# Four graph layers in one kernel: the softmax denominators of layer 0 carried by transfers instead of a matmul, and another order of the opening

## The chip, the cores and the metric

The kernel runs on one core of a Trainium2 chip. A core has TensorE (PE: matmuls, with PEld for its weight loads), VectorE (DVE), ScalarE (ACT), GpSimd (POOL) and SyncE (SP), each with its own instruction stream, executed in order, and 16 DMA engines that all queues share. The streams meet only through semaphores. The metric is device time in microseconds (us) for one execution. Lower is better.

## The reference

`x` is 4096 x 256, `adj` is a 4096 x 4096 weighted adjacency matrix, in which most entries are zero. Four layers follow one another, each with a residual and a layer norm:

```python
x = _layernorm(x + attention(x, adj))      # layer 0: 4 heads of 64, below
x = _layernorm(x + gat(x, adj))            # layer 1: masked softmax over neighbours
x = _layernorm(x + gcn(x, adj))            # layer 2: normalized adj @ x @ W.T + b
x = _layernorm(x + relu(gcn3(x, adj)))     # layer 3
# layer 0, per head:
scores = q @ k.T * HD ** -0.5 + graph_bias * adj
scores = where(adj == 0, -1e9, scores)
attn   = exp(scores - max) / sum(exp(scores - max))
out    = attn @ v            # heads side by side, then @ Wout + bout
```

The change concerns layer 0 alone. All data are float32, except a bfloat16 copy of the adjacency that layer 0 writes for layer 1.

## The kernel before, in words

Layer 0 treats the queries in 32 blocks of 128 rows (class `Rows`) and each block in two units, one per pair of heads (class `Pair`). A unit takes 4 steps of 1024 keys each, so there are 64 units and 256 steps. The function `step(t)` writes out by hand what each engine does in step t; inside `manual_schedule` the order of the program is the order on each engine. A software pipeline lays the stages of a unit over several steps. In step t:

- `score` (L366, PE): the scores of the current unit into two PSUM tiles `sc`; DVE adds the bias and takes the row maximum (`z`, L375).
- `expo` (L391, ACT): exponentials of the unit four steps back, with the row sums collected in `ls`.
- `turn` (L405, PE; copied out by ACT, L413): the exponentials are transposed by TensorE, five steps back.
- `attend` (L423, PE): values times transposed exponentials, six steps back, into the PSUM tile `po`: 64 channels of head 0 on partitions 0 to 63, of head 1 on 64 to 127, queries along the free axis.
- `make_bias` and `make_edges`: for the next block of queries, DVE turns a tile of the adjacency (`raw`, loaded by SP in four transfers, L256) in 32 x 32 blocks (L272) and makes the bias from it (L277, L278); ACT makes the bfloat16 copy (L289) and POOL sends it to DRAM (`edge`, L295). There are two `raw` buffers.

With `ka` for the step of the unit that attends (0 to 3), a unit ends like this. The sums lie one per partition (a query is a partition in `ls`), but `po` has the queries along the free axis, so the reciprocals must be turned and repeated over 64 partitions. In step ka = 2 `sums` reduces `ls`, takes the reciprocals and spreads them over 64 columns each (`lb`, L437, DVE). In step ka = 3, after `attend`, `norm` multiplies `lb` by the identity on TensorE (L441) into a PSUM tile `pb`, which DVE copies to `rb` (L449). At the start of the next step (ka = 0 of the next unit) `scale` multiplies `po` by `rb` into `oT` (L452). For every second unit, step ka = 1 runs `finish`: output projection (L335), residual and layer norm statistics on DVE (L345, L113, L114). `begin` makes the queries of the next block (L313, PE; L321, DVE; L329, POOL) in step ka = 0 of every second unit. `po`, `pb`, the pq of `begin` and the pp of `finish` all live in two PSUM tiles, tags `po0` and `po1`.

The opening comes before step 0 and overlaps steps 0 to 3. The eight blocks of 512 rows of x are projected to keys and values by `project`: keys (L210, PE, evicted by ACT, L217), then values (L226, PE, evicted by DVE, L233). The bias of block 0 is made from four `raw` tiles. Both must have been done for the first scores. The program calls `begin` first, then interleaves the whole bias of block 0 with `project(0)` and `project(1)`, and projects two blocks at the start of each of the steps 1 to 3, ahead of the scores.

Of the kernel before, what the change touches and what calls it, by code (L numbers as in the profile page):

```python
# [16 lines left out]
P = 128  # L17
# [27 lines left out]
def tile_gnn(  # L45
# [59 lines left out]
    sc = [ps_q.tile([P, TS], F32, name=f"sc{j}") for j in range(2)]  # L105

    edge = dram.tile([N, N], BF16, name="edge")
    off_diag = const.tile([P, P], F32, name="off_diag")
    nc.vector.tensor_scalar(off_diag, ident, -1.0, 1.0, ALU.mult, ALU.add)

# [58 lines left out]
    with ExitStack() as l0:  # L169
# [31 lines left out]
            )  # L201
            x_in[mb] = xt

        def project(mb):

            xt = x_in.pop(mb)
            for pr in range(2):
                pk = ps_o.tile([P, 512], F32, tag=f"po{pr}", name="pk")
                for cc in range(2):
                    nc.tensor.matmul(  # L210
                        pk,
                        wkv_sb[:, cc, pr * P : (pr + 1) * P],
                        xt[:, cc, :],
                        start=(cc == 0),
                        stop=(cc == 1),
                    )
                nc.scalar.activation(  # L217
                    kT[:, pr, mb * 512 : (mb + 1) * 512],
                    pk,
                    AF.Identity,  # L220
                    bias=bqk_sb[:, 2 + pr : 3 + pr],
                )
            pv = ps_t.tile([P, 4, D], F32, tag="tr", name="pv")
            for s in range(4):
                for cc in range(2):
                    nc.tensor.matmul(  # L226
                        pv[:, s, :],
                        xt[:, cc, s * P : (s + 1) * P],
                        wkv_sb[:, cc, D : 2 * D],
                        start=(cc == 0),  # L230
                        stop=(cc == 1),
                    )
            nc.vector.tensor_tensor(  # L233
                v_sb[:, mb * 4 : (mb + 1) * 4, :],
                pv,
                bv_b.unsqueeze(1).to_broadcast([P, 4, D]),
                ALU.add,
            )
            if mb + 4 < N // 512:
                load_x(mb + 4)  # L240

        class Rows:

# [64 lines left out]
            def begin(self, tag):  # L308
                self.qT = wk2.tile([P, 2, P], F32, tag="qT", name="qT")
                pq = ps_o.tile([P, 512], F32, tag=tag, name="pq")  # L310
                for pr in range(2):
                    for cc in range(2):
                        nc.tensor.matmul(  # L313
                            pq[:, pr * P : (pr + 1) * P],
                            wq_sb[:, cc, pr * P : (pr + 1) * P],
                            self.xq[:, cc, :],
                            start=(cc == 0),
                            stop=(cc == 1),
                        )
                for pr in range(2):  # L320
                    nc.vector.tensor_scalar(  # L321
                        self.qT[:, pr, :],
                        pq[:, pr * P : (pr + 1) * P],
                        bqk_sb[:, pr : pr + 1],
                        HD ** -0.5,
                        ALU.add,
                        ALU.mult,
                    )
                nc.gpsimd.tensor_tensor(self.xr, self.xr, bout_b, ALU.add)  # L329
                self.oT = wk2.tile([P, 2, P], F32, tag="oT", name="oT")  # L330

            def finish(self, tag):
                pp = ps_o.tile([P, 512], F32, tag=tag, name="pp")
# [16 lines left out]
        class Pair:  # L350
# [79 lines left out]

            def sums(self):

                l2 = wk2.tile([P, 2], F32, tag="l2", name="l2")
                nc.vector.tensor_reduce(l2, self.ls, AX.X, ALU.add)
                nc.vector.reciprocal(l2, l2)
                self.lb = wk2.tile([P, 2, HD], F32, tag="lb", name="lb")
                nc.vector.tensor_copy(self.lb, l2.unsqueeze(2).to_broadcast([P, 2, HD]))  # L437

            def norm(self, tag):
                pb = ps_o.tile([P, 512], F32, tag=tag, name="pb")  # L440
                nc.tensor.matmul(  # L441
                    pb[:, 0:P],
                    self.lb.rearrange("p j d -> p (j d)"),
                    ident,
                    start=True,
                    stop=True,
                )
                self.rb = wk2.tile([P, P], F32, tag="rb", name="rb")
                nc.vector.tensor_copy(self.rb, pb[:, 0:P])  # L449

            def scale(self):
                nc.vector.tensor_tensor(  # L452
                    self.rows.oT[:, self.pr, :], self.po[:, 0:P], self.rb, ALU.mult
                )
# [7 lines left out]
        def step(t):  # L462
# [10 lines left out]
            grow = live and ib + 1 < NCH  # L473
            if grow and pr == 0 and k == NS - 1:
                rows[ib + 1].fetch()
            if ua > 0 and ka == 0:
                pairs[ua - 1].scale()
            if t > 0:
                for mb in range(2 * t, min(2 * t + 2, N // 512)):
                    project(mb)  # L480
            if live:
                if k == 0:
                    pairs[unit] = Pair(rows[ib], pr)
                pairs[unit].score(k)
            if expos:
                pairs[ue].expo(ke, 0)
            if turns:
# [3 lines left out]
            if attends:  # L491
                pairs[ua].attend(ka, tag_a)
                if ka == NS - 2:
                    pairs[ua].sums()
                if ka == NS - 1:
                    pairs[ua].norm(tag_o)
            if ua > 0 and ka == 1:
                if ua % 2 == 0:
                    pairs[ua - 1].rows.finish(tag_o)
                del pairs[ua - 1]  # L500
            if grow:
                if pr == 1 and k == NS - 2:
                    rows[ib + 1].begin(tag_o if attends else "po1")
                kb, half = divmod(pr * NS + k, 2)
                if edges:
                    edges.pop().make_edges()
                edges.append(rows[ib + 1])
                rows[ib + 1].make_bias(kb, half)
                if half == 0 and kb + 1 < NS:
                    rows[ib + 1].load(kb + 1)  # L510
                elif half == 0 and ib + 2 < NCH:
                    rows[ib + 2].load(0)
# [1 line left out]
                edges.pop().make_edges()  # L514
            if turns:
                pairs[ut].turn(kt, 1, by_dve=not live)
            for f, *args in tail.get(t, ()):
                f(*args)

# [97 lines left out]
        def first_es():  # L617
# [30 lines left out]
                (first_es,),  # L648
            ],
        }  # L650
        with tc.manual_schedule():
            load_x(0)
            nc.sync.dma_start(wkv_sb, wqkv[:, D:].rearrange("(c p) e -> p c e", p=P))
            rows[0].load(0)
            load_x(1)
            rows[0].load(1)
            rows[0].fetch()
            load_x(2)
            load_x(3)
            nc.scalar.dma_start(wout_sb, wout.rearrange("(c p) e -> p c e", p=P))  # L660
            nc.scalar.dma_start(bout_b, bout.partition_broadcast(P))
            rows[0].begin("po1")
            for k in range(NS):
                for half in range(2):
                    rows[0].make_bias(k, half)
                    rows[0].make_edges()
                if k < 2:
                    project(k)
                if k + 2 < NS:
                    rows[0].load(k + 2)  # L670
                elif k + 2 == NS:
                    rows[1].load(0)
            for t in range(n_steps + LA + 2):
                step(t)

# [444 lines left out]
```

## Time and profile before

| | |
|---|---|
| median of 3 runs | 2788.17 us (2787.74 to 2789.93) |
| the profiled execution, its own time | 2790.52 us |
| its span, first to last instruction | 2788.7 us |
| PE busy | 2720.9 us, 98% |
| DVE busy | 2225.5 us, 80% |
| ACT busy | 1655.4 us, 59% |
| POOL busy | 234.3 us, 8% |
| layer 0, roughly | 0 to 1436 us |

The page gives busy time by engine, the span in slices, the chain of work that ended last, and the costliest groups of instructions with what ended the idle time ahead of them. A timeline lists instructions with start and duration; a row of several instructions is merged. The end of a matmul is modelled, so where TensorE does one thing after another, the time from one start to the next is the safer measure.

### The profile page before, as it was taken

What the parts mean: (1) busy time and instruction counts of PE and PEld (TensorE: products, weight loads), DVE (VectorE), ACT (ScalarE), POOL (GpSimd) and SP (SyncE); (2) the same over time, 40 slices, a digit from 0 to 9 for tenths busy, and PEclk for the clock granted to TensorE, in tenths of its full rate; (3) what the DMA queues carried; (4) which work ended last, traced back from release to release, by engine and by line L of the source; (5) the groups of instructions that cost most, each with busy time, mean ns of one, the idle gap of its engine ahead of it and who ended that gap; (6) DMA issues with size and microseconds to landing.
All of it is one profiled execution on the core that took longest, in us unless ns stands there. A gap on an engine that the chain in (4) does not pass through costs nothing.

```text
span 2788.7 us, 57962 instructions
## 1 busy us (share of the span) xinstructions
PE 2720.9 (98%) x23568; PEld 1862.4 (67%) x23568; DVE 2225.5 (80%) x4059; ACT 1655.4 (59%) x2675; POOL 234.3 (8%) x404
## 2 busy tenths in 40 slices
PE   6999999999999999999997999999999999999997
PEld 4677777777777777777786888886444444444443
DVE  4799999999988999999858888885866577676565
ACT  2699999999999999999857777772100001000000
POOL 1111111111111111111100000000200000000000
PEclk9999999999999999999999999999999999999998
DMA  6344444444444444444362222212555555555552
GB/s 156 63 83 86 93 87 85 89 90 83 87 92 83 88 89 84 90 87 87 95 202 70 77 77 76 76 43 90 176 158 170 162 159 157 164 168 175 181 169 73
DMA packets 671291, 308.01 MB, mean 110 GB/s; under 512 B 547376, under 2 KB 577456, under 8 KB 671024
## 3 DMA queue, kind: packets, MB, share of 16 engines
q1 hardware_dynamic: 655776, 265.10, 38.7%
q0 software_dynamic: 13440, 37.77, 3.5%
q8 instruction: 184, 3.01, 0.5%
q10 hardware_dynamic: 1808, 1.44, 0.2%
q14 instruction: 83, 0.68, 0.1%
HBM read 258.21 MB, written 46.01 MB: 109 GB/s over the span
## 4 chain that ended last, share of the span: by engine, by line
PE 93%; issue 3%; DVE 1%; DMA 1%; ACT 1%; SPq 0%; POOL 0%; DVEq 0%; POOLq 0%; ACTq 0%
PE m L948 27%; PE po L423 17%; PE po L770 16%; PE sc L366 16%; PE ptr L405 10%; PE py L982 2%; PE pq L313 1%; PE pp L335 1%; PE pb L441 1%; PE pk L210 1%; PE pv L226 1%; DMA mk<-edge 1%; SPq L256 0%; DMA x<-xs 0%; DVE z L375 0%
## 5 line engine op out<-in xcount | busy, mean ns | idle before, releaser
L375 DVE CUSTOM_DVE_ANT_0 z<-sc,bias 128x1024 f32<-128x1024 f32 x512 | 605.9, 1221 | 40.5 <-PE sc L366 39.0
L391 ACT ACTIVATE z<-z,nm 128x1024 f32<-128x1024 f32 x512 | 590.2, 1153 | 6.7 <-DVE nm L387 6.7
L413 ACT COPY pt<-ptr 128x1024 f32<-128x1024 f32 x507 | 511.4, 1009 | 99.3 <-PE ptr L405 89.9
L366 PE MATMUL sc<-store,qT 64*128 64x512 f32 x2048 | 506.7, 608 | 1.6 <-DVE mx L375 1.5
L423 PE MATMUL po<-pt,xc 128*64 128x128 f32 x8192 | 504.2, 276 | 0.0
L770 PE MATMUL po<-store,pt 128*128 128x257 f32 x2048 | 447.2, 380 | 12.6 <-issue 12.6
L423 PEld LDWEIGHTS po<-pt,xc 128*64 128x64 f32 x8192 | 442.3, 137 | 17.6 <-DVE pt L411 0.2
L405 PEld LDWEIGHTS ptr<-ident,z 64*128 64x128 f32 x8192 | 322.3, 138 | 177.8 <-issue 78.4
L770 PEld LDWEIGHTS po<-store,pt 128*128 128x128 f32 x2048 | 388.6, 190 | 70.9 <-issue 12.7
L948 PE MATMUL m<-asum,ysum 128*128 128x512 f32 x768 | 356.6, 594 | 6.3 <-issue 6.3
L405 PE MATMUL ptr<-ident,z 64*128 64x64 f32 x8192 | 356.3, 225 | 5.8 <-ACT pt L413 4.4
L366 PEld LDWEIGHTS sc<-store,qT 64*128 64x128 f32 x2048 | 192.9, 189 | 119.4 <-issue 109.2
L948 PEld LDWEIGHTS m<-asum,ysum 128*128 128x128 f32 x768 | 146.0, 190 | 177.9 <-issue 160.9
L948 PE MATMUL m<-asum,store 128*128 128x512 f32 x512 | 263.2, 596 | 0.0
L948 PE MATMUL m<-a,ysum 128*128 128x512 f32 x512 | 245.9, 594 | 0.0
L295 POOL DMA_DIRECT2D edge<-mk x256 | 145.4, 568 | 1004.5 <-ACT mk L289 981.1
L954 ACT COPY e<-m 128x512 f32<-128x512 f32 x32 | 18.5, 586 | 351.6 <-PE m L948 351.6
L917 DVE TENSOR_TENSOR asum<-a 128x512 f32<-128x512 f32 x128 | 88.1, 688 | 163.9 <-PE m L948 163.9
L724 ACT ACTIVATE z<-z,es_q 128x1024 f32<-128x1024 f32 x128 | 146.5, 1145 | 120.5 <-DVE mx L711 111.9
L278 DVE SCALAR_TENSOR_TENSOR bias<-rt,gb,u 128x512 f32<-128x512 f32 x256 | 194.2, 759 | 9.1
L760 DVE STREAM_TRANSPOSE pt<-z 128x1024 f32<-128x1024 f32 x128 | 158.1, 1237 | 41.7 <-PE po L770 41.7
L948 PEld LDWEIGHTS m<-asum,store 128*128 128x128 f32 x512 | 97.8, 191 | 123.3 <-issue 121.4
(123 smaller groups left out, 2561.5 us busy)
## 6 DMA issues: line engine op xcount, KB each, us to landing
a<-in_adjT SPq DMA_DIRECT2D x256, 512.0 KB, 5.1
raw<-in_adjT SPq DMA_DIRECT2D x512, 128.0 KB, 4.0
edge<-mk POOLq DMA_DIRECT2D x256, 128.0 KB, 2.5
mk<-edge SPq DMA_DIRECT2D x256, 128.0 KB, 2.9
xt<-in_xT SPq DMA_DIRECT2D x8, 512.0 KB, 5.4
xq<-in_xT SPq DMA_DIRECT2D x32, 128.0 KB, 3.9
xr<-in_x SPq DMA_DIRECT2D x32, 128.0 KB, 3.1
x<-xs POOLq DMA_DIRECT2D x8, 512.0 KB, 4.1
```

The lines of the kernel that those rows point to most:

```text
L278: nc.vector.scalar_tensor_tensor(self.bias[k][:, m0 : m0 + HT], rt, gb, u, ALU.mult, ALU.add)
L295: nc.gpsimd.dma_start(edge[self.ib * P : (self.ib + 1) * P, k * TS + m0 : k * TS + m0 + HT], mk)
L366: nc.tensor.matmul(ps[j][:, q * 512 : (q + 1) * 512], self.rows.qT[j * HD : (j + 1) * HD, self.pr, :], kT[j * HD : (j + 1) * HD, self.pr, ...
L375: nc.vector.tensor_tensor_reduce(z, ps[j], self.rows.bias[k], 1.0, NEG, ALU.add, ALU.max, self.mx[:, j, k : k + 1],)
L391: nc.scalar.activation(z, z, AF.Exp, bias=self.nm[:, j : j + 1], accum_out=self.ls[:, j, k : k + 1],)
L405: nc.tensor.transpose(pa[:, r, c, :], z[half, c * P : (c + 1) * P], ident[half, half])
L413: nc.scalar.copy(to, pa)
L423: nc.tensor.matmul(self.po[j * HD : (j + 1) * HD, 0:P], v_sb[:, ci, h * HD : (h + 1) * HD], self.pt[j][k][:, c, :], start=(ci == 0), stop= ...
L724: nc.scalar.activation(self.z[s], self.z[s], AF.Prelu, bias=self.eq[:, s : s + 1], alpha=SLOPE)
L760: nc.vector.transpose(self.pt[:, :, s, :], self.z[s].rearrange("p (b r) -> p b r", r=QB))
L770: nc.tensor.matmul(self.po[:, 0 : D + 1], self.pt[:, b, :, :].rearrange("p s i -> p (s i)"), wh[:, b, :], start=(b == 0), stop=(b == NBK - 1),
L948: nc.tensor.matmul(self.m[i], left, right, start=(c == 0), stop=(c == NP - 1))
```

## The change

Three things change, all in layer 0.

1. The reciprocals. `sums` no longer widens them to 64 columns; DVE turns them in 32 x 32 blocks into `lt`, in which each group of 32 partitions has a head's reciprocals of 32 queries along the free axis in its first two rows. Two transfers on POOL's queue write these rows to a new DRAM tile `norm`, 4 rows of 128 bytes each. At the end of the same step `spread` reads them back with two more transfers, each of which repeats 128 values on 64 partitions of `rb`. `norm` with its matmul and its copy is gone.
2. `scale` moves from the start of step ka = 0 to its end. To leave `po` its PSUM tile until then, `begin` moves from step ka = 0 to step ka = 3 before it.
3. The opening. `project` is split into `project_k` and `project_v`. Ahead of step 0 stand only the keys of blocks 0 and 1, `begin`, and the first quarter of the bias. A table `plan` puts the rest into steps 0 to 4, after the step's scores: values, keys for the next step's scores, and the bias for them. The loads of `raw`, `xt` and `xq` are reordered with it.

```diff
+    norm = dram.tile([2 * NCH, 2, P], F32, name="norm")
...
-        def project(mb):
-
-            xt = x_in.pop(mb)
+        def project_k(mb):
+
+            xt = x_in[mb]
...
+        def project_v(mb):
+
+            xt = x_in.pop(mb)
...
-            if mb + 4 < N // 512:
-                load_x(mb + 4)
+            if mb + 5 < N // 512:
+                load_x(mb + 5)
...
-                self.oT = wk2.tile([P, 2, P], F32, tag="oT", name="oT")
...
             def sums(self):
 
+                u = 2 * self.rows.ib + self.pr
                 l2 = wk2.tile([P, 2], F32, tag="l2", name="l2")
                 nc.vector.tensor_reduce(l2, self.ls, AX.X, ALU.add)
                 nc.vector.reciprocal(l2, l2)
-                self.lb = wk2.tile([P, 2, HD], F32, tag="lb", name="lb")
-                nc.vector.tensor_copy(self.lb, l2.unsqueeze(2).to_broadcast([P, 2, HD]))
-
-            def norm(self, tag):
-                pb = ps_o.tile([P, 512], F32, tag=tag, name="pb")
-                nc.tensor.matmul(
-                    pb[:, 0:P],
-                    self.lb.rearrange("p j d -> p (j d)"),
-                    ident,
-                    start=True,
-                    stop=True,
-                )
+
+                lt = wk2.tile([P, QB], F32, tag="lt", name="lt")
+                nc.vector.transpose(lt, l2.unsqueeze(1).to_broadcast([P, QB // 2, 2]))
+                for j in range(2):
+                    nc.gpsimd.dma_start(
+                        norm[u, j, :].rearrange("(a c) -> a c", c=QB),
+                        lt.rearrange("(a r) c -> a r c", r=QB)[:, j, :],
+                    )
+
+            def spread(self):
+
+                u = 2 * self.rows.ib + self.pr
                 self.rb = wk2.tile([P, P], F32, tag="rb", name="rb")
-                nc.vector.tensor_copy(self.rb, pb[:, 0:P])
+                for j in range(2):
+                    nc.gpsimd.dma_start(
+                        self.rb[j * HD : (j + 1) * HD, :], norm[u, j, :].partition_broadcast(HD)
+                    )
 
             def scale(self):
+                if self.pr == 0:
+                    self.rows.oT = wk2.tile([P, 2, P], F32, tag="oT", name="oT")
...
-            if ua > 0 and ka == 0:
-                pairs[ua - 1].scale()
-            if t > 0:
-                for mb in range(2 * t, min(2 * t + 2, N // 512)):
-                    project(mb)
             if live:
...
                 pairs[unit].score(k)
+            for f, *args in plan.get(t, ()):
+                f(*args)
...
-                if ka == NS - 1:
-                    pairs[ua].norm(tag_o)
...
-                if pr == 1 and k == NS - 2:
+                if pr == 1 and k == NS - 3:
                     rows[ib + 1].begin(tag_o if attends else "po1")
...
-                if half == 0 and kb + 1 < NS:
+                if t < NS:
+
+                    if t == 1:
+                        rows[0].load(3)
+                    if 0 < t < 3:
+                        rows[1].load(t)
+                elif half == 0 and kb + 1 < NS:
                     rows[ib + 1].load(kb + 1)
...
                 pairs[ut].turn(kt, 1, by_dve=not live)
+            if attends and ka == NS - 2:
+                pairs[ua].spread()
+            if ua > 0 and ka == 0:
+                pairs[ua - 1].scale()
...
+        def first_bias(k, half):
+            rows[0].make_bias(k, half)
+            rows[0].make_edges()
+            if k == 1 and half == 1:
+                rows[0].load(2)
+
+
+        plan = {}
+        for t in range(3):
+            plan[t] = [
+                (project_v, 2 * t),
+                (project_k, 2 * t + 2),
+                (first_bias, t + 1, 0),
+                (project_v, 2 * t + 1),
+                (project_k, 2 * t + 3),
+                (first_bias, t + 1, 1),
+            ]
+        plan[3] = [(project_v, 6)]
+        plan[4] = [(project_v, 7)]
         with tc.manual_schedule():
             load_x(0)
             nc.sync.dma_start(wkv_sb, wqkv[:, D:].rearrange("(c p) e -> p c e", p=P))
             rows[0].load(0)
+            rows[0].fetch()
             load_x(1)
             rows[0].load(1)
-            rows[0].fetch()
-            load_x(2)
-            load_x(3)
+            for mb in range(2, 5):
+                load_x(mb)
             nc.scalar.dma_start(wout_sb, wout.rearrange("(c p) e -> p c e", p=P))
             nc.scalar.dma_start(bout_b, bout.partition_broadcast(P))
+            project_k(0)
             rows[0].begin("po1")
-            for k in range(NS):
-                for half in range(2):
-                    rows[0].make_bias(k, half)
-                    rows[0].make_edges()
-                if k < 2:
-                    project(k)
-                if k + 2 < NS:
-                    rows[0].load(k + 2)
-                elif k + 2 == NS:
-                    rows[1].load(0)
+            project_k(1)
+            for half in range(2):
+                rows[0].make_bias(0, half)
+                rows[0].make_edges()
+            rows[1].load(0)
             for t in range(n_steps + LA + 2):
                 step(t)
```

## The prediction

> **What bounds the kernel now.** I read the page first: busy time by engine, then the chain that ended last.
>
> ```profile
> PE 2720.9 (98%) x23568; PEld 1862.4 (67%) x23568; DVE 2225.5 (80%) x4059; ACT 1655.4 (59%) x2675; POOL 234.3 (8%) x404
> PE 93%; issue 3%; DVE 1%; DMA 1%; ACT 1%; SPq 0%; POOL 0%; DVEq 0%; POOLq 0%; ACTq 0%
> ```
>
> TensorE carries 93% of the chain, so a matmul removed from layer 0 should shorten it, if nothing else in the step is as long. To see that, I took the timeline of TensorE in the middle of layer 0, through one step with the matmul that goes (L441).
>
> ```profile
> 1009.29 0.71 PE L405 MATMUL ptr<-ident,z 64*128 64x64 f32 x16
> ...
> 1012.20 1.97 PE L423 MATMUL po<-pt,xc 128*64 128x128 f32 x32
> 1014.09 0.49 PE L441 MATMUL pb<-ident,lb 128*128 128x128 f32 x2
> 1014.51 0.71 PE L405 MATMUL ptr<-ident,z 64*128 64x64 f32 x16
> ```
>
> From transposition to transposition a plain step takes 1014.09 - 1009.29 = 4.80 us, and L441 puts 1014.51 - 1014.09 = 0.42 us between two steps. TensorE goes from one matmul to the next without a wait. Then the busy times of whole steps (columns: stretch, length, busy time of PE, PEld, DVE, ACT, POOL, granted clock, DMA share, GB/s):
>
> ```profile
> 1009.29:1014.09 4.80, 4.80 (x74) 3.56 (x72) 4.66 (x11) 4.80 (x9) 0.55 (x1) 1.00 0.26 60
> 1014.09:1019.32 5.23, 5.23 (x76) 3.86 (x75) 4.73 (x10) 4.92 (x9) 1.28 (x2) 1.00 0.47 90
> 1041.27:1046.07 4.80, 4.80 (x74) 3.55 (x72) 4.17 (x8) 4.80 (x9) 0.54 (x1) 1.00 0.63 134
> ```
>
> ACT looks as full as PE, which would make it the bound once L441 is gone. But in the step after L441, where ACT has room, its timeline shows waits for PE of 0.17 us ahead of the copies of L413, and PE still takes 1019.32 - 1014.51 = 4.81 us. So 4.80 is TensorE's own; ACT needs about 0.1 us less. DVE has 0.1 to 0.6 us to spare. A block of two units takes 8 x 4.80 + 2 x 0.42 + `begin` 1.09 + `finish` 1.06 + 0.16 (one score behind DVE) = 41.55 us, which agrees with the distance of its `xr` additions (L329, 1015.98 to 1057.56).
>
> Last, the chain through the opening:
>
> ```profile
> 16.22 3.93 DMA xq<-in_xT
> 20.20 2.07 PE pq L313 x8
> ...
> 41.61 4.62 DMA edge<-mk
> ...
> 94.19 3.79 PE sc L366 x6
> 98.01 1.23 DVE z L375
> ```
>
> TensorE does nothing before 20.20, because `begin` comes first and its `xq` was issued at 16.22, behind two `raw` loads; it stands still for a second time around 46 (a buffer of `mk` not yet sent); and by 98.01 it has done eight projections, 8 x (3.43 + 3.45) = 55 us of work, and six scores. From 86.5 to 98 DVE and the filling pipeline bound it, with TensorE idle or slow, while all projections were squeezed in before.
>
> **What the Trainium skill says.** DMA: Bandwidth & Descriptors, Anatomy of one DMA, gives a transfer from GpSimd about 2.0 us of fixed time, most of it the receipt of the write. The trace agrees; it lists for `edge`, 128 KB from POOL:
>
> ```profile
> DMA to landing us min/median/max: 2.2/2.5/5.1
> ```
>
> The same page, Two DMAs through the same engine are not ordered, says that a read of what another transfer wrote must wait for its semaphore; so POOL must stand at the first read until the write has landed. No run here shows such a pair yet. SBUF — State Buffer, Who interferes with whom, says that GpSimd and a VectorE instruction in a two-port mode block each other, whoever comes second. Here it is milder for transfers:
>
> ```profile
> 1037.36 0.69 POOL L295 DMA_DIRECT2D edge<-mk  x1 [4.42 <-ACT mk L289]
> 1037.51 0.43 DVE L277 TENSOR_SCALAR u<-rt 128x512 f32<-128x512 f32 x1
> ```
>
> The issue grows from 0.54 to 0.69 and L277 keeps its 0.43. Only the real POOL arithmetic of L329 stretches L277 to 1.45 (at 1015.56). TensorE: Matmul & The Clock Gate, The HAM clock gate, has the array at half speed when cold; the first matmuls of pq take 0.42 us instead of 0.275.
>
> **The change part by part.**
>
> *Matmul L441 and its copy.* Removed from PE: 64 x 0.42 = 26.9 us. The last two stand in the closing steps, where DVE and ACT wait in turns, so I count 62 x 0.42 = 26.0. From DVE go 0.227 (L437) and 0.292 (L449) per unit and its waits for pb, 18.0 us in all; that is off the bound, worth nothing by itself.
>
> *Turning, on DVE.* A 128 x 32 transposition is not in the trace; 128 x 512 takes 0.702 and 128 x 1024 takes 1.237 us, a line through these gives 0.17 + 0.03 = 0.20 us. At worst 0.3. DVE's balance stays negative, 0.2 against 0.52, so no cost; DVE's idle time covers it.
>
> *Four transfers.* POOL issues 4 x 0.54 = 2.2 us more per unit of 20 us, and is 8% busy. What counts is when `rb` lands. With the times above: `sums` ends at 1009.9; writes are issued until 1011.1 and land by 1013.1 at 2.5 us; an edge issue lies between; the reads are issued at about 1012.6 and 1013.3 and land by 1015.8. `scale` now stands behind the bias of step ka = 0, at about 1021.5, or 10.6 us after `sums` in the unit without `begin`. The chain needs 0.55 + 2.5 + 0.7 + 0.55 + 2.5 = about 6.5 us, which leaves 4 us. Behind the waiting POOL stand the edge issue of the next step (4.8 us later, not reached) and, in every second unit, L329, whose result `finish` needs two steps later. Cost 0; the lower bound is a small gain of DVE time where L329 no longer meets L277 (about 1 us per block, not on the chain); the upper bound is under the rivals.
>
> *`scale` and `begin` moved.* Same instructions, same PE time (1.09 us per `begin`). `begin`'s wait of DVE for pq (0.23 us) takes the place of its wait for pb (0.43). `scale`, 0.28 us, moves one step down, where DVE has 0.56 us before the next score. Cost 0; if DVE's room is gone there, up to 0.2 x 64 = 13 us.
>
> *Closing steps.* The last `scale` needs `rb` at about 1432 to 1434; sums at 1425.8 plus 6.5 gives 1432.5, and PE is busy with L593 until 1434.3. 0 to +2.
>
> *Opening.* Worked through with the old durations: keys 3.43, values 3.45, scores 1.92 us, a landing of 4 us for `raw` and 5.5 for `xt`. `xt` 0 and the weights have landed by 8, so keys 0 run from 8 to 12.3 (cold). SP issues `raw` 0 until 11.0 as before, then `xq` at 11.0 (lands at 15), `xr`, and `xt` 1 at 12.5 instead of 11.0 (lands at 18). pq 15 to 17, keys 1 18 to 22, score 0 at 22.3. From there a step is score, two values, two keys = 15.7 us, which is also the old distance of scores (54.76 to 70.65): scores at 22.3, 38, 54 and 70 against the old 86.5 for score 3. Two values are still to do (6.9 us), but go into steps 3 and 4, where the old kernel left TensorE waiting: they take 5.4 us each instead of 3.3 and 4.3. Score 5's z comes at about 84 against 98.01: 14 us. `raw` is the risk: its third tile is freed at 37.6, lands at about 44 and is wanted at 45; the fourth lands at 62 and is wanted at 61.5. A late tile holds DVE, and behind it an eviction that TensorE needs about 4 us later. I take off 2 us for such stalls: -12, from -16 to -3.
>
> Sum on the profiled execution: 2790.5 - 26.0 - 12 = 2752.5. Its time lies 2.35 us above the median of the runs, so on the median it is 2788.2 - 38 = **2750 us**.
>
> **Rivals.**
>
> *B, the opening gives little.* Loads of `raw` collide, score 3 comes at 80 or later. For it: the landings above meet their use within 1 us, and the old opening lost time to exactly such waits. Against: 4 us of slack behind each. Then 2788.2 - 26 - (0 to 5) = 2757 to 2762.
>
> *C, another engine takes over the steady state.* ACT is 4.80 of 4.80 busy, DVE 4.66 in step ka = 2. If half of L441's time is waited for elsewhere, 2788.2 - 13 - 12 = 2763. Against: the 0.17 us waits of ACT, and 2.15 us of `begin` and `finish` per block in which ACT catches up.
>
> *D, slower: the transfers land late.* Then DVE stands at `scale`, the z behind it is late, and the next score waits for `sc`. It starts when a landing takes about 4.7 us instead of 2.5, both ways; each further microsecond costs, after 0.56 us of DVE's room, 64 us. The gain of 38 us is eaten at about 5.3 us per landing, and at 6 us the time is 2788 - 38 + 64 x 1.3 = 2833. For it: loads of `raw` of the same size as `edge` land in 4.0 us in the middle, with DMA engines 44% busy; the longest `edge` took 5.1. Against: the median of 2.5 from this queue.
>
> **How the numbers follow.** Both parts as worked out (A): 0.65, from 2743 to 2756. B 0.18, C 0.09, D 0.08. About 0.2% (5.6 us) is what a measurement of this kernel can tell from no change. A, B and C are all faster by more; a mild D or a bad C can end within it. Faster 0.90, within 0.02, slower 0.08. The range takes A, most of B and half of C: 2740 to 2764.
>
> **What would show it.** Right: plain steps of 4.80 us in a row with nothing between `po` and `ptr`; a block of about 40.7 us; no wait of DVE for `rb`; TensorE's first matmul near 8 us; score 5's z near 84 us. Wrong: DVE idle ahead of the product of `scale` with a transfer as releaser (D); waits of PE for ACT or DVE growing by as much as L441 took (C); DVE waiting for `raw` between 40 and 65 us (B).

## The result, and the profile after

The changed kernel takes 2745.46 us (median of 4 runs, 2743.03 to 2746.63); the kernel before took 2788.43 us beside it (2787.74 to 2789.93). The ratio is 0.9844, with an interval of 0.9827 to 0.9861: 43.0 us faster, where 38 were predicted, and inside the predicted range of 2740 to 2764. The profiled execution took 2743.03 us (span 2741.3), the shortest of the four; the profiled one of before took 2790.52, above its median. So the difference between the two traces is 47.5 us, 4.5 more than between the medians; places are read from the traces, the sum from the medians.

The page of after: busy times, shares of the chain by engine, and the new row of transfers (size, median us from issue to landing).

```profile
PE 2688.6 (98%) x23440; PEld 1840.8 (67%) x23440; DVE 2183.8 (80%) x3995; ACT 1648.0 (60%) x2675; POOL 379.4 (14%) x660
...
PE 96%; DVE 2%; issue 1%; DMA 1%; ACT 1%; SPq 0%; POOL 0%; DVEq 0%; ACTq 0%; POOLq 0%
...
rb<-norm POOLq DMA_DIRECT2D x128, 32.0 KB, 2.4
```

TensorE has 128 passes fewer (two per float32 matmul, 64 matmuls) and 32 us less to do; its share of the chain has grown from 93 to 96%, because time in which it stood still is gone too ("issue", waits for nothing that the profile shows, fell from 3 to 1%). POOL has 145 us more, and 256 instructions more, four in each of 64 units.

The timeline of TensorE in the middle of layer 0 (columns as before: start, length, engine, line, operation). L410 is the transposition of L405 before, L428 the `attend` of L423.

```profile
1005.29 0.71 PE L410 MATMUL ptr<-ident,z 64*128 64x64 f32 x16
...
1008.20 1.97 PE L428 MATMUL po<-pt,xc 128*64 128x128 f32 x32
1010.10 0.71 PE L410 MATMUL ptr<-ident,z 64*128 64x64 f32 x16
...
1014.90 0.71 PE L410 MATMUL ptr<-ident,z 64*128 64x64 f32 x16
```

Transpositions follow at 4.81 and 4.80 us, and nothing stands between `po` and the next `ptr`. The median distance of blocks (from one output projection to the next) fell from 41.58 to 40.74 us, which is 2 x 0.42.

Where 400 us of the steady state stand, before and after (columns: stretch, length, busy time of PE, PEld, DVE, ACT, POOL, granted clock, DMA share, GB/s):

```profile
800.00:1200.00 400.00, 400.00 (x5689) 302.41 (x5686) 364.21 (x716) 373.22 (x615) 60.17 (x107) 1.00 0.44 87
```

```profile
800.00:1200.00 400.00, 400.00 (x5780) 303.30 (x5777) 359.02 (x709) 378.69 (x628) 103.01 (x182) 1.00 0.46 93
```

TensorE is busy without a gap in both. DVE does less although more steps fit in; ACT has gained 5.5 us and stands at 94.7%.

Then the new transfers, in two views of after. First the timeline of POOL in one unit with `begin`; brackets give the idle time ahead and what ended it.

```profile
1011.42 0.54 POOL L301 DMA_DIRECT2D edge<-mk  x1 [4.25 <-ACT mk L295]
1015.80 1.20 POOL L446 DMA_DIRECT2D norm<-lt  x2 [3.84 <-DVE lt L444]
1016.99 0.58 POOL L301 DMA_DIRECT2D edge<-mk  x1
1017.95 1.07 POOL L456 DMA_DIRECT2D rb<-norm  x2 [0.37 <-issue]
```

The writes are issued when DVE has turned the reciprocals, an edge goes between, and the reads follow. Second, the timeline of DVE in the same unit:

```profile
1015.30 0.21 DVE L444 STREAM_TRANSPOSE lt<-l 128x32 f32<-128x32 f32 x1
...
1027.48 0.28 DVE L463 TENSOR_TENSOR oT<-po,rb 128x128 f32<-128x128 f32 x1
```

From the start of the turning (1015.30) the issue of the second read ends after 3.72 us, and `scale` (L463) begins after 12.18 us, with no wait. Over all units, by the same two timelines, the second read's issue ends a median of 4.31 us after the turning began in units with `begin` and 4.60 in the others, and `scale` begins after 12.18 and 10.73. An issue takes 0.55 us and a landing 2.4 us from its start, so `rb` is there at 4.60 - 0.55 + 2.4 = about 6.5 us (over all 64 units the measured landing has a median of 6.5 too), and about 4 us of slack are left. Before the reads POOL waits until the writes have landed, 53.7 us in 45 waits. The unit 20 us earlier is one of the exceptions: its writes had landed by 999.1, the reads went out only at 1002.30, they took 4.9 and 4.7 us, and DVE waited a little. What held POOL there the profile doesn't name.

```profile
1002.30 1.09 POOL L456 DMA_DIRECT2D rb<-norm  x2 [3.62 <-issue]
```

```profile
996.44 0.21 DVE L444 STREAM_TRANSPOSE lt<-l 128x32 f32<-128x32 f32 x1
...
1007.62 0.29 DVE L463 TENSOR_TENSOR oT<-po,rb 128x128 f32<-128x128 f32 x1 [0.37 <-DMA rb<-norm]
```

DVE's waits for `rb` in all steps of layer 0 but the opening and closing ones (total, times, longest):

```profile
DVE oT L463 <- DMA rb<-norm: 3.3, 3, 1.6
```

**The opening.** Timeline of TensorE before, where the scores (L366) show the steps:

```profile
36.69 1.99 PE L366 MATMUL sc<-store,qT 64*128 64x512 f32 x8
...
47.68 3.70 PE L210 MATMUL pk<-xt,wkv_sb 128*128 128x512 f32 x8 [1.92 <-ACT store L217]
...
54.76 1.99 PE L366 MATMUL sc<-store,qT 64*128 64x512 f32 x8
...
86.54 1.99 PE L366 MATMUL sc<-store,qT 64*128 64x512 f32 x8
89.84 4.12 PE L366 MATMUL sc<-store,qT 64*128 64x512 f32 x8 [1.32 <-DVE mx L375]
94.19 4.07 PE L366 MATMUL sc<-store,qT 64*128 64x512 f32 x7 [0.23 <-DVE mx L375]
```

And after (scores are L371, keys L212, values L232):

```profile
7.96 6.47 PE L212 MATMUL pk<-xt,wkv_sb 128*128 128x512 f32 x8 [7.96 <-DMA wkv_sb<-in_wqkv]
15.21 1.16 PE L319 MATMUL pq<-xq,w_sb 128*128 128x128 f32 x8 [0.78 <-ACT store L219]
16.56 3.70 PE L212 MATMUL pk<-xt,wkv_sb 128*128 128x512 f32 x8 [0.19 <-DMA xt<-in_xT]
20.19 1.99 PE L371 MATMUL sc<-store,qT 64*128 64x512 f32 x8
...
36.08 1.99 PE L371 MATMUL sc<-store,qT 64*128 64x512 f32 x8
...
67.85 1.99 PE L371 MATMUL sc<-store,qT 64*128 64x512 f32 x8
69.77 3.72 PE L232 MATMUL pv<-wkv_sb,xt 128*128 128x256 f32 x16
73.42 1.99 PE L371 MATMUL sc<-store,qT 64*128 64x512 f32 x8
75.34 3.72 PE L232 MATMUL pv<-wkv_sb,xt 128*128 128x256 f32 x16
78.99 1.99 PE L371 MATMUL sc<-store,qT 64*128 64x512 f32 x8
```

Score 0 starts 16.5 us earlier, score 3 18.7 us (86.54 to 67.85). Each step has two instructions `z` on DVE; I count by the first of a step. That of score 5 starts at 82.11 instead of 98.01, that of the ninth step ("the ninth `z`") at 96.15 instead of 114.15: 18.0 us. The first L441 of the old kernel comes only after that, at 121.24. The last output projection of layer 0 starts at 1389.48 instead of 1434.31, 44.8 us earlier; the rest, 44.8 - 18.0 = 26.8 us, is 64 x 0.42. At the first large matmul of layer 2 (1893.2 against 1937.7) the gain is still 44.5; the last 3 us of the difference between the two traces arise in layers 2 and 3, which the change doesn't touch. From that matmul to the end the trace of before takes 851.1 us and that of after 848.1, but a run below that leaves those layers as they were (transfers beside) takes 847.8. So this is scatter, not the change.

### The profile page after: what moved, and what is told of

Read it like the earlier page. It is cut to its first block, busy times and chain, and to the rows that moved or that the text cites. A ratio compares the mean times of both kernels' runs of the same rounds, so it can differ in the third digit from the quotient of the medians.

```text
span 2741.3 us, 58184 instructions
## 1 busy us (share of the span) xinstructions
PE 2688.6 (98%) x23440; PEld 1840.8 (67%) x23440; DVE 2183.8 (80%) x3995; ACT 1648.0 (60%) x2675; POOL 379.4 (14%) x660
## 3 DMA queue, kind: packets, MB, share of 16 engines
q10 hardware_dynamic: 1808, 1.44, 0.2%
## 4 chain that ended last, share of the span: by engine, by line
PE 96%; DVE 2%; issue 1%; DMA 1%; ACT 1%; SPq 0%; POOL 0%; DVEq 0%; ACTq 0%; POOLq 0%
PE m L980 27%; PE po L428 18%; PE sc L371 16%; PE po L802 16%; PE ptr L410 11%; PE py L1014 2%; PE pp L340 1%; PE pq L319 1%; PE pv L232 1%; PE pk L212 1%; PE sc L139 1%; DMA xt<-in_xT 0%; SPq L262 0%; DMA rb<-norm 0%; DVE pt L416 0%
## 5 line engine op out<-in xcount | busy, mean ns | idle before, releaser
L428 PE MATMUL po<-pt,xc 128*64 128x128 f32 x8192 | 504.1, 276 | 0.0
L371 PE MATMUL sc<-store,qT 64*128 64x512 f32 x2048 | 502.9, 604 | 0.1
L428 PEld LDWEIGHTS po<-pt,xc 128*64 128x64 f32 x8192 | 442.1, 137 | 17.5 <-DVE pt L416 0.2
L410 PEld LDWEIGHTS ptr<-ident,z 64*128 64x128 f32 x8192 | 322.0, 138 | 178.4 <-issue 82.5
L410 PE MATMUL ptr<-ident,z 64*128 64x64 f32 x8192 | 356.6, 225 | 4.5 <-ACT pt L418 3.2
L371 PEld LDWEIGHTS sc<-store,qT 64*128 64x128 f32 x2048 | 192.7, 188 | 116.7 <-issue 109.8
L278 DVE STREAM_TRANSPOSE rt<-raw 128x512 f32<-128x512 f32 x256 | 179.9, 703 | 0.3 <-issue 0.3
```

The source lines that it names most:

```text
L278: nc.vector.transpose(rt.rearrange("p (b r) -> p b r", r=QB), self.raw_now[:, half * nb : (half + 1) * nb, :],)
L371: nc.tensor.matmul(ps[j][:, q * 512 : (q + 1) * 512], self.rows.qT[j * HD : (j + 1) * HD, self.pr, :], kT[j * HD : (j + 1) * HD, self.pr, ...
L410: nc.tensor.transpose(pa[:, r, c, :], z[half, c * P : (c + 1) * P], ident[half, half])
L428: nc.tensor.matmul(self.po[j * HD : (j + 1) * HD, 0:P], v_sb[:, ci, h * HD : (h + 1) * HD], self.pt[j][k][:, c, :], start=(ci == 0), stop= ...
```

## The experiments

**The two parts alone.** The first has the opening, with L441, its copy, `scale` and `begin` as before.

```diff
 # the kernel before, and from the change only: project_k and project_v, plan, the order of loads
```

> The opening alone: the kernel before with project_k, project_v, plan and the new order of loads; the matmul L441, its copy, scale and begin stay where they were. Theory (the two parts simply add on TensorE's path: 18 us from the opening, 26.9 us from the matmul): 2788.4 - 18 = 2770 us, the ninth z of layer 0 near 96 us instead of 114, the blocks of queries still 41.6 us apart. Rival (the opening's gain needs begin one step earlier, since begin then falls into a step in which TensorE has room): 2 us less of it, 2772 to 2773 us.

Measured: 2772.98 us, ratio 0.9941 (0.9926 to 0.9956), 15.3 us less than the 2788.28 of before beside it. In its trace the block stays at 41.58 us and the ninth `z` starts at 97.86, 1.7 us later than with both parts: the rival's number came (the interval holds the theory's 2770 too, the trace decides). Of the 1.7 us, 0.6 are a later start (`xt` 1 landed at 17.1), and 1.1 is `begin` for the second block, which here stands between two full steps (from `z` to `z` 5.58 us there, 4.57 with both parts).

The second has the transfers, with the old opening.

```diff
 # the changed kernel, with project, the order of loads and the opening of before
```

> The reciprocals by transfers, with scale and begin moved, but the old opening. Theory: 64 x 0.42 = 26.9 us less, 2788.4 - 26.5 = 2762 us, blocks 40.7 us apart. Rival (the transfers or the later scale cost something in the steady state, which a larger gain of the opening hides in the sum): 2765 us or more, and then the opening alone gives more than 20 us.

Measured: 2762.87 us, ratio 0.9903 (0.9888 to 0.9917), 25.4 us less. The block takes 40.74 us, the ninth `z` starts at 115.93, the last output projection at 1408.62. The theory held. What follows: only the transfers shorten the block, and the new order does its work in the opening; the two sum to 40.7 us against 43.0 for both, within what the runs scatter. 25.4 us over 62 units is 0.41 us each: all of L441's time came back, and rival C (half of it waited for elsewhere) falls. No run moved `scale` and `begin` alone, but plain steps take 4.80 us before and after, so the block leaves nothing for that move to explain.

**What one matmul costs.**

```diff
-                nc.tensor.matmul(
+                for _ in range(2):
+                    nc.tensor.matmul(
...
```

> The kernel before with the matmul L441 issued twice into the same pb, so that the same values come out. It prices the matmul by itself. Theory: it stands on TensorE's path with nothing beside it, so a second one costs what the first does, 64 x 0.42 = 27 us: 2815 us. Rival (part of its time is the wait for lb or the turn-around of pb, which a second one doesn't pay again): 10 to 20 us, 2798 to 2808 us.

Measured: 2803.76 us, ratio 1.0051 (1.0036 to 1.0066), 15.5 us more, or 0.24 us for each of 64. Timeline of TensorE of this kernel, where the pair is L442:

```profile
1022.18 1.97 PE L423 MATMUL po<-pt,xc 128*64 128x128 f32 x32
1024.08 0.71 PE L442 MATMUL pb<-ident,lb 128*128 128x128 f32 x4
1024.72 0.71 PE L405 MATMUL ptr<-ident,z 64*128 64x64 f32 x16
```

Two take 1024.72 - 1024.08 = 0.64 us where one took 0.42, so the second costs 0.22. The other 0.20 us is paid once per unit. The rival in the expectation held in its number, not the doubling. Its reason is not shown: the profile has no wait for `lb` or `pb` ahead of L441, and what the 0.20 us consists of, a change from one stream of matmuls to another form or something else, stays open. The Trainium skill (TensorE: Matmul & The Clock Gate, Single matmul latency) puts a single warm bf16 matmul that nothing overlaps at a constant of about 166 ns over its stream; 0.20 us is of that size, but no run here tells whether it is the same thing.

**What turning and transfers cost beside the old way.** DVE turns the reciprocals and POOL issues the four transfers, but nobody reads the tile they fill; `pb` and its copy stay. The reads repeat 32 values instead of 128, so they move 8 KB each instead of 32.

```diff
+                lt = wk2.tile([P, QB], F32, tag="lt", name="lt")
+                nc.vector.transpose(lt, l2.unsqueeze(1).to_broadcast([P, QB // 2, 2]))
+                for j in range(2):
+                    nc.gpsimd.dma_start(
+                        norm[u, j, :].rearrange("(a c) -> a c", c=QB),
+                        lt.rearrange("(a r) c -> a r c", r=QB)[:, j, :],
+                    )
...
+            def spread(self):
...
+                for j in range(2):
+                    nc.gpsimd.dma_start(
+                        idle[j * HD : (j + 1) * HD, :], norm[u, j, 0:QB].partition_broadcast(HD)
+                    )
...
```

> The kernel before with the turning and the four transfers added per unit, while the matmul still makes the reciprocals: the transfers land in a tile that nobody reads, and the reads bring 32 of the 128 values. Theory (issue on POOL and the transfers themselves are hidden, 0.21 us of DVE per unit fits its room): 2788 to 2791 us. Rival (four more descriptors writes per unit hold DVE, or the loads of the adjacency land later): 64 x 0.1 to 0.3 = 6 to 20 us, 2795 to 2808 us.

Measured over 12 runs: 2788.74 us, ratio 0.9999 (0.9990 to 1.0008). The same 400 us of its trace:

```profile
800.00:1200.00 400.00, 400.00 (x5688) 302.38 (x5684) 364.68 (x736) 373.25 (x615) 103.73 (x184) 1.00 0.44 88
```

TensorE and ACT do what they did before; POOL has its 43 us more, DVE hardly more. The cost of nothing that the prediction gave to turning and issues is shown, to within about 2.8 us (reads of the full 32 KB stand only in the runs that use them). By the Trainium skill (SBUF — State Buffer, Who interferes with whom) POOL and a DVE instruction in a two-port mode block each other; with twice as many issues on POOL, the mean length of L277 (L278 in this kernel) over these 400 us is 521 ns, and 520 before, so the new issues did not do that to it. Whether L277 runs in such a mode, no run shows.

**How much slack stands behind `scale`.** Three runs take it away. In the first, `scale` goes back to the start of step ka = 0, about 4 us earlier; `begin` stays where the change put it.

```diff
+            if ua > 0 and ka == 0:
+                pairs[ua - 1].scale()
             if live:
...
-            if ua > 0 and ka == 0:
-                pairs[ua - 1].scale()
```

> The changed kernel with scale back at the start of the step, ahead of the score's z, as it was with the matmul; begin stays moved. It asks what the later scale is worth. After sums, rb lands after about 5.8 us where the writes land in 1.8, and after about 9 us where they take 4 to 6; scale's place is then 5.7 to 6.1 us after sums in a unit without begin, 6.8 us with it. Theory (DVE waits for rb in the slow third of the units for about 2.5 us beyond its room of 0.5 us): 10 to 50 us slower than the changed kernel, 2755 to 2795 us, with DVE waiting for the transfer in 15 to 40 of 64 units. Rival (the place of scale doesn't matter, as the transfers are in time either way): 2745 us, no such waits.

Measured: 2772.25 us, ratio 0.9936 (0.9920 to 0.9953): 16.9 us faster than before beside it, so some 26 us of the gain are lost. (In the profiled execution the opening began 2.9 us later besides.) The waits of its steady steps (total, times, longest; PE and PEld are two queues of one engine, and PE's 10.7 us lie within PEld's 19.4):

```profile
DVE oT L463 <- DMA rb<-norm: 34.3, 18, 5.9
PEld sc L371 <- DVE mx L380: 19.4, 19, 4.0
PE sc L371 <- DVE mx L380: 10.7, 5, 3.9
```

This is the chain that rival D described: DVE stands at `scale`, the maximum behind it is late, and TensorE waits for it with the next score. From the ninth `z` to the last output projection this trace takes 1322.3 us, the changed kernel's 1293.3. All late units are without `begin`: there `scale` now comes 6.3 us after the turning, with `begin` ahead of it 8.0 us, and with some 6.5 us for the way about half of the former are late (19 of 34, with the closing) and none of the 30 others. The largest three waits, 4.9 to 5.9 us, belong to the three units in which the reads' issue ended 6.9 to 8.5 us after the turning: in one the writes took over 5 us, in one the second write went out late and landed after 3.8, and in one both writes had landed in under 2 us, but the reads went out 3.6 us late and took 4.7 to 4.8. The expectation's numbers held, its reason (slow writes alone) did not: the usual way is already as long as the place allows.

The other two leave `scale` where the change has it and lengthen the way: the values go through one more, or two more, DRAM tiles before they are spread.

```diff
+                src = norm
+                for hop in hops:
+                    nc.gpsimd.dma_start(hop[u], src[u])
+                    src = hop
...
-                        self.rb[j * HD : (j + 1) * HD, :], norm[u, j, :].partition_broadcast(HD)
+                        self.rb[j * HD : (j + 1) * HD, :], src[u, j, :].partition_broadcast(HD)
```

> The changed kernel with one more transfer in the chain: norm is copied in DRAM to a second tile, and rb is read from that. Theory: a hop adds an issue of 0.55 us and a landing of about 2.5 us, so rb lands about 9 us after sums in the fast units, still ahead of scale at 10.6, and about 12 in the slow third, 1 to 1.5 us late, with DVE's room of 0.5 us: 5 to 25 us slower than the changed kernel, 2750 to 2770 us. Rival (the slack is larger than worked out, or DVE's wait is hidden by TensorE): within 3 us of it.

Measured: 2771.63 us, ratio 0.9935 (0.9920 to 0.9950), 25.5 us of the gain lost, just past the upper end of what was expected. DVE waits for `rb` 24.9 us in 16 units, of which 8.8 us in the closing steps. That doesn't account for all: some blocks without such a wait are 0.2 to 0.5 us longer too, and why stays open.

> The changed kernel with two more transfers in the chain. Theory (past the slack each microsecond of lateness costs a microsecond per unit, 64 us in all): rb lands about 12 us after sums in the fast units and 15 in the slow ones, on average some 2 us late against 10.6, less 0.5 us of DVE's room: 64 x 1.5 to 2.5 = 95 to 160 us slower, 2840 to 2905 us. Rival (late transfers are absorbed over the following steps, in which DVE catches up before TensorE needs it): under 40 us slower.

Measured: 2834.34 us, ratio 1.0162 (1.0147 to 1.0177), 88 us more than the changed kernel. The waits of its steady steps:

```profile
DVE oT L468 <- DMA rb<-hop: 88.0, 46, 4.6
...
PEld sc L372 <- DVE mx L381: 38.3, 46, 2.7
...
PE sc L372 <- DVE mx L381: 13.7, 10, 2.5
```

A hop costs POOL 0.5 us of issue and a wait of 2.0 to 2.5 us for the landing (115.2 and 147.0 us in 59 each in this trace), so about 3 us. With one, 48 of the 64 units are in time, and all but one of the late are without `begin`; the second puts 46 late. So the slack is between one hop and two, as the 4 us of the trace say. The end pays less than DVE waits, 88 us for 113 us in 50 units (whole run), because the first part of each wait is free. Twelve of the seventeen blocks with a single wait show how much: from one output projection to the next they are longer by that wait less 0.64 to 0.72 us (waits of 1.94, 2.15 and 4.62 us, blocks longer by 1.23, 1.44 and 3.91); the other five lose more. With the early `scale`, ahead of the bias, the free part is 0.37 to 0.43 us in twelve of sixteen (a wait of 1.13 us, 0.70 longer). So the price that D named, 1:1 past 0.56 us of room, roughly holds: with 0.56 us taken off each wait, 86.7 of the 113 us are left. The expectation of 95 to 160 us was too high because it gave all units the 10.6 us of a unit without `begin`; with it `scale` comes after 12.4 us here, and only 15 of those units are among the 50.

**Parts of the opening.** First, all values before score 3: blocks 6 and 7 are done at the end of step 2.

```diff
-        plan[3] = [(project_v, 6)]
-        plan[4] = [(project_v, 7)]
+        plan[2] += [(project_v, 6), (project_v, 7)]
```

> The changed kernel with the last two value projections at the end of step 2, ahead of the fourth score, instead of in steps 3 and 4. Theory (in steps 3 to 5 VectorE sets the pace and TensorE has room for them): the fourth score comes 6.9 us later, steps 3 and 4 get shorter by some 3.5 us in all, so 3 to 4 us of the opening's 18 us are lost: 2748 to 2749 us, the ninth z at 99 to 100 us instead of 96.15. Rival (all of the opening's gain comes from the earlier start, and where the values stand is indifferent): the ninth z stays at 96 us.

Measured: 2752.82 us, ratio 0.9868 (0.9853 to 0.9883), 6.7 us of the gain lost, twice what was expected. Timeline of TensorE:

```profile
73.32 3.72 PE L232 MATMUL pv<-wkv_sb,xt 128*128 128x256 f32 x16 [1.32 <-DVE xc L239]
76.97 1.99 PE L371 MATMUL sc<-store,qT 64*128 64x512 f32 x8
81.37 4.23 PE L371 MATMUL sc<-store,qT 64*128 64x512 f32 x8 [2.41 <-DVE mx L380]
```

The values come in a row, so the second waits 1.32 us for DVE's eviction of the first, and score 4 waits 2.41 us for DVE, as in the old opening. Measured from the first `z`, the ninth comes 80.7 us later instead of 73.9: 6.8 us, as much as the two projections take (6.9). That is what this part of the plan is worth. The expectation had steps 3 and 4 give back half of it; they did get shorter, by 3.1 us, but the `z` of score 3 came 9.6 us later (from the first `z`), not 6.9.

Second, the load of `xq` goes back behind both `raw` tiles.

```diff
             rows[0].load(0)
-            rows[0].fetch()
             load_x(1)
             rows[0].load(1)
+            rows[0].fetch()
```

> The changed kernel with the load of xq back where it was, behind the first two tiles of the adjacency and xt 1. It asks how much of the opening's 18 us hangs on that one load. Theory (TensorE executes in order, so keys 1 stand behind begin, and begin behind xq, which lands at 20.2 us as in the kernel before): the first score at 25 instead of 20.2 us, all later steps shifted with it, the ninth z at 101 us, 2750 us in all. Rival (a later start is caught up in steps 0 to 4): ninth z at 96 to 97 us, 2745 us.

Measured: 2749.93 us, ratio 0.9852 (0.9836 to 0.9869); by the intervals it can't be told from the changed kernel. The trace tells more. TensorE of this kernel:

```profile
7.97 6.67 PE L212 MATMUL pk<-xt,wkv_sb 128*128 128x512 f32 x8 [7.97 <-DMA wkv_sb<-in_wqkv]
20.16 2.04 PE L319 MATMUL pq<-xq,w_sb 128*128 128x128 f32 x8 [5.52 <-issue]
22.00 4.72 PE L212 MATMUL pk<-xt,wkv_sb 128*128 128x512 f32 x8
26.65 1.99 PE L371 MATMUL sc<-store,qT 64*128 64x512 f32 x8
```

pq starts 5.0 us later, where SP's issue of `xq` has moved behind `xt` 1 and the four transfers of a `raw` tile, and takes 2.04 instead of 1.16 us, and keys 1 take 4.72 instead of 3.70, after a gap of 5.5 us in which TensorE had nothing to do. Score 0 and the ninth `z` come 6.5 us later. That is the theory's account, and the rival (a later start is caught up) falls: at the last output projection this execution is still 8.0 us behind. The median moved by 4.5 only; nothing was given back within this execution, so the rest looks like scatter between executions.

**Two steps further.** The step after `finish` still took 4.96 us in the changed kernel: the score there is late, because the residual on DVE waits for the projection (0.88 us) ahead of the bias. Here `finish` is split, and its DVE half goes behind the bias and `scale`.

```diff
+                self.pp = pp
+
+            def residual(self):
+                pp = self.pp
...
-                    pairs[ua - 1].rows.finish(tag_o)
+                    done = pairs[ua - 1].rows
+                    done.finish(tag_o)
...
+            if done:
+                done.residual()
```

> The changed kernel with finish split: the output projection stays, its residual and statistics on VectorE move to the end of the step, behind the next bias, so that VectorE no longer idles for the matmul ahead of the bias. In the trace of the changed kernel the step after each finish takes TensorE 4.96 instead of 4.80 us. Theory (that is VectorE's 0.88 us of waiting, which makes its z late): 31 x 0.16 = 5 us less, 2740 us. Rival (VectorE is just as late with the work moved, since the work is the same): no change, 2745 us.

Measured: 2741.88 us, ratio 0.9833 (0.9819 to 0.9846), 2 us from the theory. Timeline of TensorE in the step that had 4.96 us:

```profile
986.91 0.71 PE L414 MATMUL ptr<-ident,z 64*128 64x64 f32 x16
...
991.71 0.71 PE L414 MATMUL ptr<-ident,z 64*128 64x64 f32 x16
992.26 1.94 PE L375 MATMUL sc<-store,qT 64*128 64x512 f32 x8
...
996.51 0.71 PE L414 MATMUL ptr<-ident,z 64*128 64x64 f32 x16
```

4.80 us. The block is 40.58 us, and the 31 distances from the first to the last output projection sum to 1252.15 instead of 1256.33 us: 4.2 us gained in the trace, which the medians' intervals alone would not show.

Last, on top of that the loads of `xt` 1, `xq` and `xr` go ahead of the first `raw` tile.

```diff
-            rows[0].load(0)
-            rows[0].fetch()
             load_x(1)
+            rows[0].fetch()
+            rows[0].load(0)
             rows[0].load(1)
```

> The kernel with the split finish, and the loads of xt 1, xq and xr ahead of the first tile of the adjacency. In the changed kernel TensorE waits from 14.4 to 16.56 us for xt 1. Theory: keys 1 start at 14.5, the first z then waits for the first bias, which comes about as before; 1 to 2 us less than the kernel with the split finish alone. Rival (the first tile of the adjacency becomes the bound and lands later by as much): no change or 1 to 3 us more.

Measured: 2737.94 us (2737.81 to 2740.08), ratio 0.9819 (0.9806 to 0.9832); the best of all, 3.9 us under the run before it, with intervals that overlap, and 7.5 us under the changed kernel. TensorE:

```profile
14.19 1.16 PE L319 MATMUL pq<-xq,w_sb 128*128 128x128 f32 x8 [0.78 <-ACT store L219]
15.18 3.60 PE L212 MATMUL pk<-xt,wkv_sb 128*128 128x512 f32 x8
18.71 1.99 PE L375 MATMUL sc<-store,qT 64*128 64x512 f32 x8
```

Score 0 starts at 18.71 us; with the split `finish` alone it was 20.68, and the ninth `z` moved by as much, from 96.64 to 94.67: 2.0 us, the upper end of the theory. Keys 1 now follow pq at once, where they had waited 1.37 us for `xt` 1; pq waits for the keys' eviction, as before.

## Why the prediction was right

- *Matmul L441, -26.0.* Right in size and place. The trace gives 26.8, the part alone 25.4. That only 0.22 of its 0.42 us are paid again by a second one doesn't matter, since all of it goes with the matmul.
- *Turning, 0.20 us.* The line through the two longer transpositions held: the group of after has a mean of 212 ns.

```profile
L444 DVE STREAM_TRANSPOSE lt<-l 128x32 f32<-128x32 f32 x63 | 13.3, 212 | 2.4 <-DVE l L441 0.3
```

- *Four transfers, 0, with 4 us of slack.* Right: `rb` is there about 6.5 us after the turning, and `scale` comes at 10.7 or 12.2. That the figure itself was met is in part luck: its terms sum to 6.8, and its times (1009.9 to 1015.8) give 5.9. The sign "no wait of DVE for `rb`" did not come quite true: there were four, 5.4 us in all, and the three in steady steps made their blocks 0.6, 1.0 and 0 us longer. The Trainium skill's 2.0 us for a transfer from GpSimd (DMA: Bandwidth & Descriptors, Anatomy of one DMA) stands beside medians of 1.8 us for the writes and 2.4 for the reads; the trace adds the spread, up to 6.0 and 4.9. The run with transfers beside the old way prices them at nothing, the runs with hops show the edge.
- *`scale` and `begin` moved, 0.* Right in the sum, wrong in one size: I let `begin`'s wait of DVE for pq stay at 0.23 us, and it is 1.10 (33.0 us in 30). DVE had the room: score and transposition after it are on time.
- *Closing, 0 to +2.* Within it: one wait for `rb` of 2.1 us in the closing steps, of which 0.5 us reached the projection.
- *Opening, -12.* The term that was mis-sized: 18.0 us in the trace, 15.3 in the run with this part alone. Three amounts (1.9, 2 and 2.1) add up to the 6 us. `xt` 1 landed at 16.5 instead of 18, and keys 1 took 3.6 us instead of 4.3, so score 0 started at 20.2 instead of 22.3, although keys 0 took 6.5 us cold where I had 4.3. (The distance of scores was then 15.89 us, as of old; the 15.7 of the working were 0.2 short.) The early landing is in part luck of this execution: in the six other runs with this order of loads it came at 17.0 to 17.7, and score 0 at 20.7 to 23.1. The 2 us that I took off for stalls behind `raw` were not lost: DVE waited for no `raw` tile there. The 14 us up to score 5 were 15.9. And I stopped counting at score 5, while the next three steps gave another 2.1 us. Of these 1.1 belong to the move of `begin`, which for the second block now falls into step 5, where TensorE has room, and no longer between two full steps: from score 5's `z` to the ninth it is 16.14 us before, 15.04 with the transfers alone, 15.14 with the opening alone, 14.04 with both. The other 1.0 comes with the new order; what in it does this, no run shows.
- *Rivals.* B is excluded by the landings, C by the part alone, D by the waits. D's mechanism is real, as two hops show: it needs about 4 us more on the way, and but for single units they were not there. Its sum has a slip: if both landings get longer, each microsecond of landing makes `rb` two later, so by its own terms the gain would be eaten at about 5.0 us per landing, not 5.3, and 6 us would give about 2916 us, not 2833.

## What to carry to other kernels

A value that TensorE turns or spreads only for its layout can go by DRAM instead, if its consumer can be put far enough behind: take the way from the issue rows and landings of the same queue in the profile, take the slack from the timeline, and give the consumer room for the slow units, not for the median alone. Where TensorE is the bound, a lone small matmul between two streams can be worth more than its own stream (here 0.42 us, where a second one cost 0.22). In an opening, count which transfer the first matmul of each kind waits for, and spread work that is not needed yet over steps in which the bound engine stands idle.

## What the runs showed of the hardware

- A lone float32 matmul of 128x128 between two streams of other forms cost 0.42 us, a second one behind it 0.22 us.
- A round trip from SBUF to DRAM and back over POOL's queue, with DMA engines 46% busy, took about 6.5 us from the start of the producing instruction (0.2 us), in single units up to 12.0: two issues of 0.59 us, a landing of 1.8 us (1.6 to 6.0), two issues of 0.55 us, a landing of 2.4 us (2.3 to 4.9).
- The first eight matmuls of keys took 5.4 to 6.7 us where they came first on TensorE, against 3.6 later; after a gap of 5.5 us with nothing to do and pq, 4.72 us, and in one execution (early `scale`) 5.40 us after two gaps of 1.6 us.
- With 43 us more of transfer issues on POOL in 400 us, DVE's L277 kept its mean length (521 ns, 520 before).
